# Two changes of shape: the bias network's second layer in column tiles, and self-attention without weight products

## The chip, the cores and the metric

The kernel runs on one core of a Trainium2 chip. The time is that of the device, in microseconds, and the time given for a kernel is the median of its runs. Everything is computed in 32-bit floats. TensorE multiplies matrices: it holds one operand (the weights[...]) and streams the other past it (here mostly 512 columns), and writes into PSUM, a memory of 8 banks of 128 partitions by 512 floats. VectorE (DVE), ScalarE (ACT) and GpSimd (POOL) do the other arithmetic, SyncE (SP) starts most transfers. Each engine works through its own queue[...].

## The reference

The input is x, two images of 512 channels by 32x32 points (1024 points). Two blocks follow one another. The first is a deformable attention with eight heads (groups) in each image, thus 16 pairs of image and head; each head has 64 channels and 64 sampled keys. What matters here is the bias that a small network computes for each pair of a query point (1024) and a key (64):

```
pos  = grid_q[:, :, None, :] - grid_kv[:, None, :, :]        # 2 numbers a pair
bias = sign(pos) * log1p(abs(pos))
bias = relu(bias @ cpb_w1 + cpb_b1)                          # 2 -> 128
bias = relu(bias @ cpb_w2 + cpb_b2)                          # 128 -> 128
bias = bias @ cpb_w3 + cpb_b3                                # 128 -> 1
sim  = (q k^T) * scale + bias
out  = softmax(sim) v                                        # then out_w, residual
```

An MLP (512 to 2048 to 512, gelu) with a residual ends the first block. The second block is self-attention over the 1024 points of an image with 512 channels and one head:

```
q, k, v = Wq x + bq,  Wk x + bk,  Wv x + bv
out     = x + Wp (softmax(q^T k / sqrt(512)) v) + bp
```

## The kernel before

It runs in five stages, all on one core: the preparation (queries, offsets, sampled keys, and the features `fea` of positions, which go to memory as `fdr` and come back spread over all partitions), the bias loop, the MLP, and the self-attention.

The bias loop is written for the 16 pairs of image and head, which the code calls groups. A step `s` deals with two keys (r and r+32 of the 64); there are 512 steps. The functions are:

- `st_tables` (L270 to L283) loads the features of 32 keys (`fb`) and makes two tables from them, `ta` on ScalarE and `tb` on GpSimd: the first layer's products with x and with y.
- `st_layer1` (L285) makes `h1`, 128 hidden units by 1024 points for one key, as the clamped sum of a column of `ta` and one of `tb`, one VectorE instruction for a key (L290). Four buffers.
- `st_layer2` (L299) multiplies `h1` by the 128x128 weights `cw2` into a tile of two banks (L304; two calls, one for each 512 points), and ScalarE takes it out with bias and relu as `h2` (L308). Three such tiles in PSUM.
- `st_layer3` (L312) sums over the 128 hidden units with `w3p` (L327). The weights are a window of 32 columns in which one column holds the weights and the rest are 0, so that each step's two keys land on their own partitions of `sim`; for two halves of the points and two keys there are four calls on four column tiles of 32. The first step of a group also multiplies queries and keys into the same bank (L317).
- `softmax_steps` (L333) turns a group's scores (`pt`, L339), normalises them on VectorE and ScalarE, turns them back (`pb`, L354) and multiplies by the values (`pa`, L361), in four parts that are spread over the loop by `due`.

The loop's order is written out by hand: in step s the first layer of step s+1, the second layer of s, and in every second step the third layer of the two steps before; a part of the softmax comes every second step. The tile framework puts the instructions in the engines' queues by the order of the text and by when it expects their inputs, so that an instruction can stand somewhat later than written, and it sets the semaphores.

The self-attention first multiplies weights by weights: `gw[0]` from Wq and Wk, `gw[1]` from Wv and Wp (`psg`, L460), and two bias vectors `ub` (`psu`, L469). Then, for each image, `qs` (`psp`, L484), values `vt` (`psv`, L493), scores against x itself (`pss`, L504), softmax, turning (`psx`, L523), and the output (`psa`, L544), which has Wp in it already.

Of the kernel before, what the change touches and what calls it, by code (L numbers as in the profile page):

```python
# [14 lines left out]
P = 128  # L15
# [5 lines left out]
R = 32  # L21
# [10 lines left out]
    ("bq", 4), ("bv", 4), ("bp", 4), ("dwb", 1), ("cb1", 1), ("cb2", 1), ("cb3", 1), ("w3", 1),  # L32
    ("w1x", 1), ("w1y", 1), ("dww", 36),
# [10 lines left out]
def conv_seq_kernel(ctx: ExitStack, tc: tile.TileContext, x, kst, cst, vec, wsm, outw, w1, w2, wl, out):  # L44
# [16 lines left out]
    def col(name, i=0):  # L61
        return vs[:, VOFF[name] + i : VOFF[name] + i + 1]
# [7 lines left out]
    w3p = cp.tile([P, 2 * R - 1], F32, name="w3p")  # L70
    nc.gpsimd.memset(w3p, 0.0)
    nc.gpsimd.tensor_copy(w3p[:, R - 1 : R], col("w3"))

    dp = ctx.enter_context(tc.tile_pool(name="dp", bufs=1, space=bass.MemoryType.DRAM))
    fdr = dp.tile([NG, 2, 2 * W, R], F32, name="fdr")
# [13 lines left out]
    with tc.tile_pool(name="ph", bufs=1) as ph, tc.tile_pool(name="ph2", bufs=2) as ph2, tc.tile_pool(  # L89
# [92 lines left out]
        for f in range(2):  # L182
# [12 lines left out]
        nc.vector.tensor_copy(  # L195
            kv.rearrange("p k b (e r) -> p (k b) r e", e=2), pk.rearrange("p (g r e) -> p g r e", r=R, e=2)
        )
# [45 lines left out]
        for c in range(2):  # L243
            nc.sync.dma_start(
                out=fdr[:, c, :, :].rearrange("g p j -> p g j"),
                in_=fea[0:64].rearrange("p f g (c j) -> p (f g) c j", c=2)[:, :, c, :],
            )
# [11 lines left out]
    with tc.tile_pool(name="lp", bufs=2) as lp, tc.tile_pool(  # L259
# [4 lines left out]
        NS = NG * R  # L264
        tabs, h1s, h2s, sims = {}, {}, {}, {}


        def st_tables(c):
            b, k, f = groups[c // 2]
            fb = lp.tile([P, 2, W, R], F32, name="fb", bufs=1)  # L270
            nc.sync.dma_start(
                out=fb.rearrange("p a x j -> p (a x j)"),
                in_=fdr[f * 8 + b * NCH + k, c % 2].rearrange("p j -> (p j)").partition_broadcast(P),
            )
            ta = lp.tile([P, R, W], F32, name="ta")
            tb = lp.tile([P, R, H], F32, name="tb")
            nc.scalar.activation(  # L277
                ta.rearrange("p j x -> p x j"), fb[:, 0], AF.Identity, bias=col("cb1"), scale=col("w1x")
            )
            nc.gpsimd.tensor_scalar(  # L280
                tb.rearrange("p j y -> p y j"), fb[:, 1], col("w1y"), 0.0, ALU.mult, ALU.add
            )
            tabs[c] = (ta, tb)  # L283

        def st_layer1(s):  # L285
            ta, tb = tabs[s // 16]
            for e in range(2):
                j = 2 * (s % 16) + e
                h1 = lp.tile([P, HW], F32, name="h1", bufs=4)
                nc.vector._custom_dve(  # L290
                    TENSOR_ADD_SAT,
                    out=h1.rearrange("p (y x) -> p y x", x=W),
                    in0=ta[:, j, :].unsqueeze(1).to_broadcast([P, H, W]),
                    in1=tb[:, j, :].unsqueeze(2).to_broadcast([P, H, W]),
                    s0=FMAX, s1=0.0,
                )
                h1s[s, e] = h1

        def st_layer2(s):  # L299
            for e in range(2):  # L300
                h1 = h1s.pop((s, e))
                ps = zp.tile([P, 2, 512], F32, name="ps2")
                for h in range(2):
                    nc.tensor.matmul(  # L304
                        ps[:, h, :], cw2, h1[:, h * 512 : (h + 1) * 512], start=True, stop=True
                    )
                h2 = lp.tile([P, 2, 512], F32, name="h2", bufs=6)
                nc.scalar.activation(h2, ps, AF.Relu, bias=col("cb2"))  # L308
                h2s[s, e] = h2

        def st_layer3(s):
            gi, r = divmod(s, R)  # L312
            b, k, f = groups[gi]
            if r == 0:
# [8 lines left out]
            h2 = [h2s.pop((s, e)) for e in range(2)]  # L323
            for h in range(2):
                for e in range(2):
                    q = 64 * h + 32 * e
                    nc.tensor.matmul(  # L327
                        sims[gi][q : q + 32, :], w3p[:, R - 1 - r : 2 * R - 1 - r], h2[e][:, h, :],
                        start=False, stop=(r == R - 1),
                    )  # L330

        def softmax_steps(gi):
            b, k, f = groups[gi]  # L333
            sim = sims.pop(gi)
            ss = lp.tile([P, 512], F32, name="ss")
# [7 lines left out]
            ex = lp.tile([P, 8, J], F32, name="ex")  # L343
# [11 lines left out]
            at = lp.tile([P, 512], F32, name="at")  # L355
# [14 lines left out]
        st_tables(1)  # L370
        st_layer1(0)
        for s in range(NS + 2):
            if s % 16 == 2 and s // 16 >= 1 and s // 16 + 1 < 2 * NG:
                st_tables(s // 16 + 1)
            if s + 1 < NS:
                st_layer1(s + 1)
            if s < NS:
                st_layer2(s)
            if s % 2 == 0 and s >= 2:
                st_layer3(s - 2)  # L380
                st_layer3(s - 1)
                if s % R == 0:
                    tail = softmax_steps(s // R - 1)
                    due = s
            if tail is not None and s >= due:
                tail = tail if next(tail, 0) is None else None
                due = s + 2
# [54 lines left out]

    wl_s = cp.tile([P, 4, NCH, C], F32, tag="big", name="wl_s")
# [4 lines left out]
    with tc.tile_pool(name="sp", bufs=1) as sp, tc.tile_pool(  # L448
        name="sps", bufs=2, space=PSUM
    ) as sps, tc.tile_pool(name="spm", bufs=4, space=PSUM) as spm:  # L450

        gw = sp.tile([P, 2, NCH, C], F32, name="gw")
        ub = sp.tile([P, 2, NCH], F32, name="ub")
        for i in range(2):
            for k in range(NCH):
                ps = spm.tile([P, 512], F32, tag="ps", name="psg")
                for o in range(NCH):
                    nc.tensor.matmul(  # L460
                        ps, wl_s[:, 2 * i, o, k * P : (k + 1) * P], wl_s[:, 2 * i + 1, o, :],
                        start=(o == 0), stop=(o == NCH - 1),
                    )
                nc.scalar.copy(gw[:, i, k, :], ps)
        for i, bn in enumerate(("bq", "bv")):
            for k in range(NCH):
                ps = spm.tile([P, 512], F32, tag="ps", name="psu")
                for o in range(NCH):
                    nc.tensor.matmul(  # L469
                        ps[:, 0:1], wl_s[:, 2 * i + 1, o, k * P : (k + 1) * P], col(bn, o),  # L470
                        start=(o == 0), stop=(o == NCH - 1),
                    )
                if i == 0:
                    nc.vector.tensor_copy(ub[:, i, k : k + 1], ps[:, 0:1])
                else:
                    nc.vector.tensor_tensor(ub[:, i, k : k + 1], ps[:, 0:1], col("bp", k), ALU.add)
        for b in range(B):
            qs = sp.tile([P, NCH, HW], F32, name="qs")
            for o in range(NCH):
                for h in range(2):  # L480
                    n = slice(h * 512, (h + 1) * 512)
                    ps = spm.tile([P, 512], F32, tag="ps", name="psp")
                    for k in range(NCH):
                        nc.tensor.matmul(  # L484
                            ps, gw[:, 0, k, o * P : (o + 1) * P], xs[:, k, b, n],
                            start=(k == 0), stop=(k == NCH - 1),
                        )
                    nc.scalar.activation(qs[:, o, n], ps, AF.Identity, bias=ub[:, 0, o : o + 1])
            vt = sp.tile([P, 8, C], F32, name="vt")
            for m in range(8):  # L490
                ps = spm.tile([P, 512], F32, tag="ps", name="psv")
                for k in range(NCH):
                    nc.tensor.matmul(  # L493
                        ps, xs[:, k, b, m * P : (m + 1) * P], gw[:, 1, k, :],
                        start=(k == 0), stop=(k == NCH - 1),
                    )
                nc.vector.tensor_copy(vt[:, m, :], ps)
            aT = sp.tile([P, 8, HW], F32, name="aT")

            def scores(t):  # L500
                ps = sps.tile([P, 2, 512], F32, name="pss")
                for h in range(2):
                    for k in range(NCH):
                        nc.tensor.matmul(  # L504
                            ps[:, h, :], qs[:, k, t * P : (t + 1) * P], xs[:, k, b, h * 512 : (h + 1) * 512],
# [32 lines left out]
            turn(7, before)  # L538
            for h in range(2):
                n = slice(h * 512, (h + 1) * 512)  # L540
                for o in range(NCH):
                    ps = spm.tile([P, 512], F32, tag="ps", name="psa")
                    for m in range(8):
# [3 lines left out]
                        )  # L547
                    res = sp.tile([P, 512], F32, name="res", bufs=3)
                    nc.vector.scalar_tensor_tensor(
                        res, ps, ub[:, 1, o : o + 1], xs[:, o, b, n], ALU.add, ALU.add  # L550
# [18 lines left out]
def _layout(np, inputs):  # L569
# [7 lines left out]
    def twice(v):  # L577
# [6 lines left out]
        "mb2": cols(L0["mlp_b2"]), "bq": cols(L1["bq"]), "bv": cols(L1["bv"]), "bp": cols(L1["bp"]),  # L584
        "dwb": twice(L0["off_dw_b"].reshape(DH, 1)), "cb1": L0["cpb_b1"].reshape(P, 1),
        "cb2": L0["cpb_b2"].reshape(P, 1), "cb3": np.broadcast_to(L0["cpb_b3"].reshape(1, 1), (P, 1)),
        "w3": L0["cpb_w3"].reshape(P, 1), "w1x": L0["cpb_w1"][0].reshape(P, 1),
# [25 lines left out]
    def rows(w):  # L613
        return w.reshape(w.shape[0] // P, P, w.shape[1]).transpose(1, 0, 2)

    wl = np.stack([rows(L1["Wq"]), rows(L1["Wk"]), rows(L1["Wv"]), lhs(L1["Wp"])], axis=1)
# [3 lines left out]
        "outw": lhs(L0["out_w"]), "w1": lhs(L0["mlp_w1"]), "w2": lhs(L0["mlp_w2"]), "wl": wl,  # L620
    }
# [20 lines left out]
```

## Time and profile before

| | |
|---|---|
| median of three runs | 3417.21 us (3415.55 to 3419.95) |
| profiled execution, its time | 3417.21 us |
| its span, first to last instruction | 3415.3 us |
| granted TensorE clock, mean | 0.990 |
| TensorE busy | 3346.8 us (98%) |
| VectorE busy | 1535.5 us (45%) |
| ScalarE busy | 1353.1 us (40%) |
| GpSimd busy | 75.7 us (2%) |
| preparation, up to the first second-layer matmul | 166.2 us |
| bias loop, up to the end of the third layer | 166.2 to 2509.9 us |
| last softmax, MLP | 2509.9 to 3020.6 us |
| self-attention | 3020.6 to 3415.3 us |

How to read it: a row of the costliest groups has the line of the code, the engine, the operation, the tile that is written and those that are read, the shape, the count, then busy time in us and the mean of one in ns, then how long the engine stood idle just before such instructions and what ended that. PE is TensorE's matmul, PEld its loading of weights, which lies beside matmuls. A shape such as `128*32 128x512` is 128 rows by 32 columns of weights, with 512 columns streamed. The mean of one matmul (about 600 ns) is longer than the time between two of them, since they are pipelined; busy time counts overlapping ones once. In a timeline a line is a start in us, a length in us, and what ran. In the chain told in order of time a line is a start, a length and a count, without the overlaps.

### The profile page before, as it was taken

To read this page: it belongs to the slowest core of one execution; us is meant where nothing else is said; L and a number is where in the kernel's file an instruction comes from. 1 tells how busy PE (TensorE), PEld (TensorE's weight loads), DVE (VectorE), ACT (ScalarE), POOL (GpSimd) and SP (SyncE) were. 2 spreads that over 40 slices of the span, in tenths; PEclk is the share of its full clock that TensorE was granted. 3 is DMA by queue.
4 is the path that set the end of the run, shared out by engine and by line. 5 is a ranking of instruction groups with operands and counts; after the bars stand their busy time and mean duration, and the time that the engine had idled before them with its cause. 6 is when DMAs were issued, how large, how long until landed. Compare 5 with 4: busy or idle time off the path is not lost.

```text
span 3415.3 us, 28243 instructions
## 1 busy us (share of the span) xinstructions
PE 3346.8 (98%) x11132; PEld 1339.9 (39%) x11132; DVE 1535.5 (45%) x1419; ACT 1353.1 (40%) x1273; POOL 75.7 (2%) x42
## 2 busy tenths in 40 slices
PE   8599999999999999999999999999999999999999
PEld 3333333333333333333333333333334444444444
DVE  2555555555555555555655555555520000002122
ACT  1355555555555555555555555555520100101010
POOL 0000000000000000000000000000000000000000
PEclk9799999999999999999999999999999999999999
DMA  1100000000000000000000000000020000100000
GB/s 63 53 25 13 13 13 13 25 13 13 13 13 13 25 13 13 13 13 13 25 13 13 13 13 13 25 13 1 1 86 0 0 0 0 49 0 0 25 0 25
DMA packets 14257, 58.77 MB, mean 17 GB/s; under 512 B 3376, under 2 KB 3632, under 8 KB 8880
## 3 DMA queue, kind: packets, MB, share of 16 engines
q1 hardware_dynamic: 13552, 55.84, 4.5%
q8 instruction: 90, 1.47, 0.2%
q10 hardware_dynamic: 576, 1.14, 0.1%
q14 instruction: 39, 0.32, 0.0%
HBM read 52.52 MB, written 4.46 MB: 17 GB/s over the span
## 4 chain that ended last, share of the span: by engine, by line
PE 98%; DVE 1%; ACT 1%; DMA 0%; issue 0%; ACTq 0%; SPq 0%; DVEq 0%
PE ps L304 53%; PE sim L327 14%; PE psm L433 6%; PE psh L425 6%; PE psa L544 3%; PE pss L504 3%; PE pc L139 2%; PE pso L409 2%; PE psp L484 2%; PE psv L493 2%; PE pa L361 1%; PE psg L460 1%; PE pkv L188 0%; PE psq L113 0%; PE sim L317 0%; PE psx L523 0%
## 5 line engine op out<-in xcount | busy, mean ns | idle before, releaser
L304 PE MATMUL ps<-h,kp 128*128 128x512 f32 x4096 | 1828.6, 599 | 12.5 <-DVE h L290 12.5
L290 DVE CUSTOM_DVE_ANT_1 h<-ta,tb 128x1024 f32<-128x1024 f32 x1024 | 1295.5, 1268 | 955.2 <-PE ps L304 943.8
L308 ACT ACTIVATE h<-ps,vs 128x1024 f32<-128x1024 f32 x1024 | 1136.1, 1113 | 1056.4 <-PE ps L304 1055.2
L304 PEld LDWEIGHTS ps<-h,kp 128*128 128x128 f32 x4096 | 756.6, 190 | 1064.6 <-issue 1050.3
L327 PE MATMUL sim<-h,w3p 128*32 128x512 f32 x4096 | 493.0, 598 | 0.0
L327 PEld LDWEIGHTS sim<-h,w3p 128*32 128x32 f32 x4096 | 107.2, 109 | 348.4 <-issue 348.1
L433 PE MATMUL psm<-hm,w_s 128*128 128x512 f32 x512 | 220.4, 592 | 0.0
L437 DVE SCALAR_TENSOR_TENSOR xs<-psm,vs,xs 128x512 f32<-128x512 f32 x16 | 12.0, 752 | 425.1 <-PE psm L433 425.1
L429 ACT ACTIVATE hm<-psh,vs 128x512 f32<-128x512 f32 x64 | 44.0, 687 | 377.7 <-PE psh L425 377.7
L425 PE MATMUL psh<-xn,w1b 128*128 128x512 f32 x384 | 165.5, 592 | 0.0
L433 PEld LDWEIGHTS psm<-hm,w_s 128*128 128x128 f32 x512 | 97.3, 190 | 122.5 <-issue 122.5
L280 POOL TENSOR_SCALAR tb<-fb,vs 128x1024 f32<-128x1024 f32 x32 | 73.7, 2302 | 2276.8 <-DVE h L290 2115.0
L504 PE MATMUL pss<-xs,qs 128*128 128x512 f32 x256 | 112.2, 592 | 0.0
L544 PE MATMUL psa<-aT,vt 128*128 128x512 f32 x256 | 111.1, 596 | 0.0
L425 PEld LDWEIGHTS psh<-xn,w1b 128*128 128x128 f32 x384 | 73.0, 190 | 91.8 <-issue 91.8
L277 ACT ACTIVATE ta<-fb,vs 128x1024 f32<-128x1024 f32 x32 | 77.5, 2421 | 36.5 <-DMA fb<-fdr 33.9
L544 PEld LDWEIGHTS psa<-aT,vt 128*128 128x128 f32 x256 | 48.9, 192 | 60.8 <-issue 60.8
L504 PEld LDWEIGHTS pss<-xs,qs 128*128 128x128 f32 x256 | 47.7, 190 | 55.5 <-issue 55.5
L514 ACT ACTIVATE ex<-pss,mx 128x1024 f32<-128x1024 f32 x16 | 17.8, 1113 | 124.6 <-DVE mx L511 124.6
L139 PE MATMUL pc<-qpad,dg 128*128 128x512 f32 x72 | 66.0, 1093 | 0.0
L409 PE MATMUL pso<-att,ow_s 128*128 128x512 f32 x128 | 58.3, 615 | 0.7 <-ACT att L365 0.7
L484 PE MATMUL psp<-xs,gw 128*128 128x512 f32 x128 | 57.0, 607 | 0.0
(102 smaller groups left out, 834.9 us busy)
## 6 DMA issues: line engine op xcount, KB each, us to landing
fb<-fdr SPq DMA_DIRECT2D x32, 1024.0 KB, 4.7
xs<-in_x SPq DMA_DIRECT2D x8, 512.0 KB, 7.7
w_s<-in_w SPq DMA_DIRECT2D x4, 1024.0 KB, 15.2
wl_s<-in_wl SPq DMA_DIRECT2D x4, 1024.0 KB, 8.0
out<-res SPq DMA_DIRECT2D x16, 256.0 KB, 2.0
w1b<-in_w SPq DMA_DIRECT2D x3, 1024.0 KB, 8.9
ow_s<-in_outw SPq DMA_DIRECT2D x1, 1024.0 KB, 6.2
w1a<-in_w SPq DMA_DIRECT2D x1, 1024.0 KB, 8.5
```

Of the source, the lines that this page charges most:

```text
L139: nc.tensor.matmul(pc.rearrange("p (g y x) -> p g y x", y=8, x=8), dg, qpad[:, :, ky : ky + 29 : 4, kx : kx + 29 : 4], start=(t == 0), sto ...
L277: nc.scalar.activation(ta.rearrange("p j x -> p x j"), fb[:, 0], AF.Identity, bias=col("cb1"), scale=col("w1x"))
L290: nc.vector._custom_dve(TENSOR_ADD_SAT, out=h1.rearrange("p (y x) -> p y x", x=W), in0=ta[:, j, :].unsqueeze(1).to_broadcast([P, H, W]), i ...
L304: nc.tensor.matmul(ps[:, h, :], cw2, h1[:, h * 512 : (h + 1) * 512], start=True, stop=True)
L308: nc.scalar.activation(h2, ps, AF.Relu, bias=col("cb2"))
L327: nc.tensor.matmul(sims[gi][q : q + 32, :], w3p[:, R - 1 - r : 2 * R - 1 - r], h2[e][:, h, :], start=False, stop=(r == R - 1),)
L409: nc.tensor.matmul(ps, ow_s[:, k, o * P : (o + 1) * P], att[:, k, b, n], start=(k == 0), stop=(k == NCH - 1),)
L425: nc.tensor.matmul(ps, w1i, xn2[:, k, :], start=(k == 0), stop=(k == NCH - 1),)
L433: nc.tensor.matmul(ps, w2_s[:, i, o * P : (o + 1) * P], hm[:, i, :], start=(i == 0), stop=(i == NF - 1),)
L484: nc.tensor.matmul(ps, gw[:, 0, k, o * P : (o + 1) * P], xs[:, k, b, n], start=(k == 0), stop=(k == NCH - 1),)
L504: nc.tensor.matmul(ps[:, h, :], qs[:, k, t * P : (t + 1) * P], xs[:, k, b, h * 512 : (h + 1) * 512], start=(k == 0), stop=(k == NCH - 1),)
L544: nc.tensor.matmul(ps, vt[:, m, o * P : (o + 1) * P], aT[:, m, n], start=(m == 0), stop=(m == 7),)
```

## The change

It does two things. In the bias loop a step now deals with two pairs of neighbouring keys. The second layer takes a pair: for each half `z` of the 128 hidden outputs (64 of them) and each half `h` of the points there are four calls with 32 columns of weights each, on four column tiles; tiles 0 and 1 stream the first key of the pair, tiles 2 and 3 the second. A bank pair of PSUM then holds 64 hidden units of the first key on partitions 0 to 63 and the same units of the second on 64 to 127. ScalarE takes the half z=0 out as `rx`, with bias and relu, and z=1 as `ry`, with bias, relu and a scale that is the size of the last layer's weight, whose sign is in `w3s`. The third layer sums `rx` with the weights `w3d` and `ry` with `w3s`, again in windows of 32 columns, with two columns filled, one for each key of the pair. A way to add `rx` and `ry` on VectorE first (`st_pair`) is in the text, but with `DIRECT = NSL` the test `paired` is never true. The tables hold 16 keys instead of 32, the features are written in four transfers instead of two, `h1` has six buffers instead of four, and the parts of the softmax come at every pair instead of every second step.

In the self-attention the products of weights go. `ks` is computed like `qs`, the scores are taken of `qs` and `ks`, the values have their bias added from `bvb`, and the output is taken out as `os_` and multiplied by Wp (`psf`).

```diff
-        def st_layer2(s):
-            for e in range(2):
-                h1 = h1s.pop((s, e))
+        def st_layer2(pair):
+            h1 = [h1s.pop((pair, t)) for t in range(2)]
+            for z in range(2):
                 ps = zp.tile([P, 2, 512], F32, name="ps2")
                 for h in range(2):
-                    nc.tensor.matmul(
-                        ps[:, h, :], cw2, h1[:, h * 512 : (h + 1) * 512], start=True, stop=True
-                    )
-                h2 = lp.tile([P, 2, 512], F32, name="h2", bufs=6)
-                nc.scalar.activation(h2, ps, AF.Relu, bias=col("cb2"))
-                h2s[s, e] = h2
+                    for q in range(4):
+                        c0 = 64 * z + 32 * (q % 2)
+                        nc.tensor.matmul(
+                            ps[32 * q : 32 * q + 32, h, :], cw2[:, c0 : c0 + 32],
+                            h1[q // 2][:, h * 512 : (h + 1) * 512], start=True, stop=True,
+                        )
+                if z == 0:
+                    rx = lp.tile([P, 2, 512], F32, name="rx", bufs=4)
+                    nc.scalar.activation(rx, ps, AF.Relu, bias=col("cb2a"))
+                else:
+                    ry = lp.tile([P, 2, 512], F32, name="ry", bufs=5)
+                    nc.scalar.activation(ry, ps, AF.Relu, bias=sc[:, 3:4], scale=sc[:, 1:2])
+            rxs[pair], us[pair] = rx, ry
...
+        def st_pair(pair):
+            if paired(pair):
...
-            h2 = [h2s.pop((s, e)) for e in range(2)]
-            for h in range(2):
-                for e in range(2):
-                    q = 64 * h + 32 * e
-                    nc.tensor.matmul(
-                        sims[gi][q : q + 32, :], w3p[:, R - 1 - r : 2 * R - 1 - r], h2[e][:, h, :],
-                        start=False, stop=(r == R - 1),
-                    )
+            for direct in (True, False):
+                if direct and paired(2 * s):
+                    continue
+                for h in range(2):
+                    for e in range(2):
+                        q = 64 * h + 32 * e
+                        src = rxs.pop(2 * s + e) if direct and h == 1 else (rxs if direct else us)[2 * s + e]
+                        nc.tensor.matmul(
+                            sims[gi][q : q + 32, :], (w3d if direct else w3s)[:, 30 - 2 * i : 62 - 2 * i],
+                            src[:, h, :], start=False, stop=(not direct and i == NSL - 1),
+                        )
...
-        for s in range(NS + 2):
...
-                due = s + 2
+        for p in range(2 * NS + 2):
+            if p % 8 == 1 and p // 8 + 1 < 4 * NG:
+                st_tables(p // 8 + 1)
+            if p + 2 < 2 * NS:
+                st_layer1(p + 2)
+            if p < 2 * NS:
+                st_layer2(p)
+            if 1 <= p <= 2 * NS:
+                st_pair(p - 1)
+            if p % 2 == 1 and p >= 3:
+                s = p // 2 - 1
+                st_layer3(s)
+                if s % NSL == NSL - 1:
+                    tail = softmax_steps(s // NSL)
+                    due = p
+            if tail is not None and p >= due:
                 tail = tail if next(tail, 0) is None else None
+                due = p + 1
...
-        gw = sp.tile([P, 2, NCH, C], F32, name="gw")
-        ub = sp.tile([P, 2, NCH], F32, name="ub")
...
+            ks = sp.tile([P, NCH, HW], F32, name="ks")
+            for i, (dst, bn) in enumerate(((qs, "bq"), (ks, "bk"))):
+                for o in range(NCH):
+                    for h in range(2):
...
+                                ps, wl_s[:, i, k, o * P : (o + 1) * P], xs[:, k, b, n],
...
-                            ps[:, h, :], qs[:, k, t * P : (t + 1) * P], xs[:, k, b, h * 512 : (h + 1) * 512],
+                            ps[:, h, :], qs[:, k, t * P : (t + 1) * P], ks[:, k, h * 512 : (h + 1) * 512],
...
+            os_ = sp.tile([P, NCH, HW], F32, tag="qs", name="os_")
...
+                    nc.scalar.copy(os_[:, o, n], ps)
+                for o in range(NCH):
+                    ps = spm.tile([P, 512], F32, tag="ps", name="psf")
+                    for k in range(NCH):
+                        nc.tensor.matmul(
+                            ps, wl_s[:, 3, k, o * P : (o + 1) * P], os_[:, k, n],
+                            start=(k == 0), stop=(k == NCH - 1),
+                        )
```

## The prediction

> **What bounds the kernel now.** I read the chain of waits, then the groups by line, and then single stretches in the timeline, in the windows and in the chain told in order of time.
>
> ```profile
> PE 98%; DVE 1%; ACT 1%; DMA 0%; issue 0%; ACTq 0%; SPq 0%; DVEq 0%
> ...
> L304 PE MATMUL ps<-h,kp 128*128 128x512 f32 x4096 | 1828.6, 599 | 12.5 <-DVE h L290 12.5
> L290 DVE CUSTOM_DVE_ANT_1 h<-ta,tb 128x1024 f32<-128x1024 f32 x1024 | 1295.5, 1268 | 955.2 <-PE ps L304 943.8
> L308 ACT ACTIVATE h<-ps,vs 128x1024 f32<-128x1024 f32 x1024 | 1136.1, 1113 | 1056.4 <-PE ps L304 1055.2
> ...
> L327 PE MATMUL sim<-h,w3p 128*32 128x512 f32 x4096 | 493.0, 598 | 0.0
> ```
>
> TensorE carries 98% of the chain, and VectorE and ScalarE spend about 950 and 1050 us waiting for L304. So only TensorE's time counts, and anything on the other engines is free until TensorE must wait for it. Each f32 matmul shows as two records (4096 for 2048 calls); I call each a pass. Three lines of the timeline, and two of the weight loads inside them from the stretch before, give the rhythm of the bias loop:
>
> ```profile
> 1526.52 7.13 PE L304 MATMUL ps<-h,kp 128*128 128x512 f32 x16
> 1533.58 1.93 PE L327 MATMUL sim<-h,w3p 128*32 128x512 f32 x16
> 1535.44 7.13 PE L304 MATMUL ps<-h,kp 128*128 128x512 f32 x16
> ...
> 1525.12 0.13 PEld L327 LDWEIGHTS sim<-h,w3p 128*32 128x32 f32 x4 [0.30 <-issue]
> 1525.55 0.13 PEld L327 LDWEIGHTS sim<-h,w3p 128*32 128x32 f32 x4 [0.30 <-issue]
> ```
>
> Four keys take 8.92 us (1526.52 to 1535.44): 16 full passes in 7.06 us, then 16 column-tile passes in 1.86 us. The weight loads of the tiles come in fours, 0.43 us apart: four column tiles run side by side in the time of one full pass. The time of one full pass, undisturbed, is in the chain in order of time:
>
> ```profile
> 2539.07 54.93 PE psh L425 x128
> ```
>
> 54.93/128 = 0.429 us. So 16 full passes and 4 groups of four would need 20 x 0.429 = 8.58 us; 0.34 us of each 8.92 is the change between the two array shapes, there and back.
>
> **What the Trainium skill says.** "TensorEngine Tiling (Array Packing)", section Key Properties, says that a change of tiling mode, not a mere change of tile, drains TensorE. The trace agrees: the 0.34 us above falls at the two changes. "TensorE: Matmul & The Clock Gate", Part 3, The mechanism, says that matmuls on different column tiles overlap, starting some 4 ns apart; the groups of four at 0.43 us agree. The Tiling page, PSUM Bottleneck, warns that tiling speeds TensorE and not evacuation. Here evacuation does not grow: two keys by 64 hidden units still fill 128 partitions, so L308's 1024 activations of 1113 ns stay 1024.
>
> **The bias loop, part by part.** Second layer: for a pair of keys 2 halves z x 2 h x 4 tiles = 16 calls, 32 passes; four keys 64 passes, 16 groups of four, 16 x 0.429. Third layer: `DIRECT = NSL` makes `paired` always false, so `st_pair` emits nothing and both `rx` and `ry` go through TensorE: 8 calls for four keys, 16 passes, 4 groups, as before. New period 8.58 us if the groups hold. There are 512/2 = 256 periods, so the shape changes give back 256 x 0.34 = 87 us.
>
> Can tiles be issued at that rate for long? 80 passes with 80 weight loads in 8.58 us is 107 ns for each pair of instructions. In the trace 211 such pairs of L188 go by in 12.43 us, 59 ns each, so issue is no bound. A burst of L327 has only four groups, so a small loss in a long run can't be excluded; nothing can be gained below 0.429. I take none, and keep +1% (22 us) as the high end; a loss beyond that is a rival.
>
> ScalarE needs 4 x 1.11 us and VectorE 4 x 1.27 us in 8.58: covered. The tables come 64 times in halves (ta about 1.25 us instead of 2.42) and their loads too: they lie in ScalarE's 1056 us and the DMA's idle time, and a chunk is asked for five pairs, some 21 us, ahead. If that cover were gone, each would cost TensorE about 4 us.
>
> **The group boundaries.** 16 times the scores of a group are turned, normalised and multiplied:
>
> ```profile
> 607.86 1.92 PE ps L304 x4
> 609.77 0.44 PE pt L339 x4
> 610.21 5.15 PE ps L304 x12
> ...
> 618.22 0.59 PE pb L354 x4
> ```
>
> From the first L304 (166.16) to the end of the last L327 (2509.9) a group takes 146.5 us, of which 16 x 8.92 = 142.7 is rhythm and 3.8 us boundary. Today the turning matmuls pt and pb stand next to L304 in L304's own shape. After the change their neighbours are 32 wide, so pt gains two shape changes, pb one, sim and the two pa one each; at 0.17 us (half of 0.34) that is 1.0 us. Next, pt is not placed at once: today it comes after two calls of L304, because ss must first be computed. Two calls of the new second layer are half a group of four, so the group is split and takes 2 x 0.86 instead of 0.86 us: +0.86 (nothing, if it falls between groups). Then there are two waits, because VectorE gets its work differently. Both h1 of a pair are set free together at the end of a second layer, 1.72 us before the third layer ends; two L290 of 1.23 us then hold VectorE until 0.9 us after it, and ss, today started at 0.14 us, comes 0.8 us later with pt behind it at the head of TensorE's queue: +0.8 (0 to 1). And pb, today due two steps later (8.6 us), is due at the next pair, 3.43 us of matmuls later. The chain ss, pt, mx, ex, Exp, sm, reciprocal, mult is 0.75 + 0.5 + 0.68 + 0.69 + 0.62 + 0.69 + 0.20 + 0.69 us with some 0.1 us between each, about 5.6 us, plus the 0.8; TensorE arrives about 5.9 us after the third layer: +0.6 (0 to 3). Behind pb wait the next pair's second layer and with it both other engines. Sum 1.0 + 0.9 + 0.8 + 0.6 = 3.3 us; bounds 0.8 to 5.5. Times 16: +53 us (13 to 88). The loop: -87 + 53 = -34.
>
> **The self-attention.** The weight products go, K and the output projection come back.
>
> ```profile
> 3020.58 27.73 PE psg L460 x64
> 3048.31 8.72 PE psu L469 x64
> 3057.03 29.21 PE psp L484 x64
> ...
> 3048.00:3057.00 9.00, 9.00 (x66) 8.85 (x64) 1.10 (x7) 0.58 (x1) 0.00 (x0) 0.80 0.01 2
> 3057.00:3061.00 4.00, 4.00 (x7) 1.76 (x7) 0.16 (x1) 0.00 (x0) 0.00 (x0) 0.60 0.00 0
> ```
>
> Removed: psg 27.73 us, psu 8.72, and what psu leaves behind: in the windows the granted clock (the column after POOL) falls to 0.80 and 0.60, and the first psp takes 29.21 where 64 x 0.429 = 27.47, so 1.74. Sum 38.2. Added for each image: ks, 8 tiles x 4 calls x 2 passes = 64 passes, 27.5 us; psf, 64 passes, 27.5 us; both images 109.9. They are on TensorE's path and nothing hides them. Net +71.7. Costed at nothing: the evictions to ks (0.69 us each, under 3.4 us of matmuls), the bias in vt (about 0.7 us as today), the load of bvb, and os_: the first three k of psf can run while its last quarter is copied. If dependencies are kept for the whole tile it costs under 1 us, four times at most.
>
> **The start.** Four writes of the features rather than two on SP (0.67 us of issue each), then a table load of half the size (perhaps 3.3 us, now 4.7) and half a ta (1.2 less); but the first group of four needs both h1 of the pair, 1.27 us more. Zero, within 3 us. The new scale columns are a few VectorE instructions of 0.17 us during the first loads.
>
> **Sum.** The profiled execution took 3417.21 us, which is also the median (span 3415.3 and 1.9 around it). -34 + 72 = +38: 3455 us.
>
> **Rivals.** (a) The boundaries grow little. The change is -15 + 16g, with g the growth of a boundary in us. With g between 0.5 and 1.4 it is within 0.2%, which is about what can be told from no change: 3417. For: TensorE's order is not fixed by the text (pt stands later than written), so an order without splits and waits is possible. Against: the shape changes alone are near 1.0. (b) The other side: faster. One mechanism: drains at the boundaries are as cheap as beside L304 today, so g stays below 0.5 and the 87 us outweighs the 72: 3402. Against: it needs pt and pb to cost nothing extra in a 32-wide neighbourhood. (c) Four streams don't keep 0.429 in long runs, for instance as two tiles read the same key at once, which no row shows: at 0.44 us a group it is 256 x 20 x 0.011 = 56 us more, 3511. (d) The passes of a call can't be grouped across four tiles in the second layer and only two run at once: 256 x 16 x 0.429 = 1757 more, 5210. L327 has the same call order and is grouped, so this is unlikely.
>
> **How the numbers follow.** The forecast 0.63, (a) 0.14, (b) 0.09, (c) 0.10, (d) 0.04. The forecast's own range is 3425 to 3485 (boundaries +21 to +76, the rest within a few us). The whole range reaches to the middle of (b) and (a) and to the nearer part of (c): 3412 to 3500. Faster is (b), 0.09; within 0.2% is (a), 0.14; the rest, 0.77, is slower.
>
> **What would show it.** A period of four keys of 8.58 us, with no gap between the second layer and the third; the second layer's weight loads in fours; group periods near 144 us with TensorE waits before pt and pb; 64 more passes for ks and psf in each image at 27.5 us. A period over 8.7 us would make (c) right; group periods under 141.5 us would make (b) right.

## The result, and the profile after

| | median | runs | ratio to before (95% interval) |
|---|---|---|---|
| before | 3417.32 us | 4 (3415.55 to 3419.95) | |
| after | 3444.78 us | 4 (3443.77 to 3445.3) | 1.0079 (1.0062 to 1.0097) |

The changed kernel is 27.5 us slower, 0.8%. The forecast was 38 us slower. The page of the changed kernel has these chain shares and groups:

```profile
PE 98%; DVE 1%; ACT 1%; DMA 0%; issue 0%; SPq 0%; ACTq 0%; DVEq 0%
...
L327 PE MATMUL ps<-h,kp 128*32 128x512 f32 x16384 | 1834.3, 593 | 12.1 <-DVE h L306 12.1
L306 DVE CUSTOM_DVE_ANT_1 h<-ta,tb 128x1024 f32<-128x1024 f32 x1024 | 1210.4, 1223 | 1012.0 <-PE ps L327 994.4
...
L333 ACT ACTIVATE rx<-ps,vs 128x1024 f32<-128x1024 f32 x512 | 570.0, 1113 | 704.5 <-PE ps L327 704.5
L336 ACT ACTIVATE ry<-ps,sc 128x1024 f32<-128x1024 f32 x512 | 614.7, 1201 | 246.3 <-PE ps L327 245.6
L366 PE MATMUL sim<-rx,w3d 128*32 128x512 f32 x2048 | 275.8, 593 | 0.0
L366 PE MATMUL sim<-ry,w3s 128*32 128x512 f32 x2048 | 275.5, 592 | 0.0
```

TensorE still bounds everything: 98% of the chain, and the other engines wait for L327. The second layer has four times the passes, 16384, in nearly the same busy time (1834.3 us, before 1828.6). That busy time is no measure of the gain: records are longer than the time between two starts, so busy time hides how closely they follow. The rhythm shows it. From the timeline of the changed kernel (start, length, what ran), first TensorE, then some of its weight loads:

```profile
1531.03 7.05 PE L327 MATMUL ps<-h,kp 128*32 128x512 f32 x64
1537.90 1.04 PE L366 MATMUL sim<-rx,w3d 128*32 128x512 f32 x8
1538.76 1.04 PE L366 MATMUL sim<-ry,w3s 128*32 128x512 f32 x8
1539.62 7.05 PE L327 MATMUL ps<-h,kp 128*32 128x512 f32 x64
...
1536.61 0.13 PEld L327 LDWEIGHTS ps<-h,kp 128*32 128x32 f32 x4 [0.30 <-issue]
1537.04 0.13 PEld L327 LDWEIGHTS ps<-h,kp 128*32 128x32 f32 x4 [0.30 <-issue]
1537.47 0.13 PEld L366 LDWEIGHTS sim<-rx,w3d 128*32 128x32 f32 x4 [0.30 <-issue]
1537.90 0.13 PEld L366 LDWEIGHTS sim<-rx,w3d 128*32 128x32 f32 x4 [0.30 <-issue]
```

Four keys take 8.59 us from start to start (8.583 as the mean of the whole periods in the trace), where 8.92 were needed. The fours of loads keep their 0.43 us across the border between the second and the third layer; nothing is lost there any more.

Where the rest went is at the group boundaries. The changed kernel's chain told in order of time, over one boundary:

```profile
599.97 1.29 PE sim L366 x12
601.26 1.70 PE ps L327 x10
602.96 0.59 PE pt L380 x4
603.54 6.14 PE ps L327 x54
609.68 1.00 PE sim L353 x2
610.68 0.59 PE pb L395 x4
611.27 1.00 PE sim L353 x2
612.27 1.85 PE sim L366 x16
614.12 1.00 PE pa L402 x2
615.12 3.57 PE ps L327 x32
618.69 1.00 PE pa L402 x2
619.69 3.57 PE ps L327 x32
```

There is no wait in it. But `pt` comes after five calls (10 passes) of the second layer, which is one group of four and one call alone, and `pb` stands between the two `sim` calls. In the kernel before, the two `sim` calls stood together:

```profile
615.36 1.01 PE sim L317 x4
```

There both took 1.01 us; here each takes 1.00 us. From one `pt` to the next the kernel before needs 146.53 us and this one 143.89 (the first and the last period apart). With the rhythm taken off (16 x 8.92 = 142.7 and 16 x 8.583 = 137.33) a boundary costs 3.83 us before and 6.56 after: it grew by 2.73 us.

By stages of the two profiled executions: from the first second-layer matmul to the self-attention's first matmul 2854.4 us before (166.16 to 3020.58) and 2807.8 after (167.29 to 2975.12), 46.6 less; the preparation 1.1 more; the self-attention 73.7 more.

### The profile page after: what moved, and what is told of

The parts are those of the page before. It is cut to its first block, busy times and chain, and to the rows that moved or that the text cites. A ratio compares the mean times of both kernels' runs of the same rounds, so it can differ in the third digit from the quotient of the medians.

```text
span 3443.5 us, 52325 instructions
## 1 busy us (share of the span) xinstructions
PE 3374.8 (98%) x23548; PEld 1200.9 (35%) x23548; DVE 1449.5 (42%) x1417; ACT 1411.5 (41%) x1329; POOL 81.7 (2%) x79
## 4 chain that ended last, share of the span: by engine, by line
PE 98%; DVE 1%; ACT 1%; DMA 0%; issue 0%; SPq 0%; ACTq 0%; DVEq 0%
PE ps L327 52%; PE sim L366 13%; PE psm L476 6%; PE psh L468 6%; PE psa L567 3%; PE psp L505 3%; PE pss L525 3%; PE pc L152 2%; PE pso L452 2%; PE psf L575 2%; PE psv L514 2%; PE pa L402 1%; PE sim L353 1%; PE pkv L201 0%; PE psq L126 0%; PE psx L544 0%
## 5 line engine op out<-in xcount | busy, mean ns | idle before, releaser
L327 PE MATMUL ps<-h,kp 128*32 128x512 f32 x16384 | 1834.3, 593 | 12.1 <-DVE h L306 12.1
L306 DVE CUSTOM_DVE_ANT_1 h<-ta,tb 128x1024 f32<-128x1024 f32 x1024 | 1210.4, 1223 | 1012.0 <-PE ps L327 994.4
L327 PEld LDWEIGHTS ps<-h,kp 128*32 128x32 f32 x16384 | 557.6, 110 | 1222.1 <-issue 1197.2
L333 ACT ACTIVATE rx<-ps,vs 128x1024 f32<-128x1024 f32 x512 | 570.0, 1113 | 704.5 <-PE ps L327 704.5
L336 ACT ACTIVATE ry<-ps,sc 128x1024 f32<-128x1024 f32 x512 | 614.7, 1201 | 246.3 <-PE ps L327 245.6
L366 PE MATMUL sim<-rx,w3d 128*32 128x512 f32 x2048 | 275.8, 593 | 0.0
L366 PE MATMUL sim<-ry,w3s 128*32 128x512 f32 x2048 | 275.5, 592 | 0.0
L525 PE MATMUL pss<-ks,qs 128*128 128x512 f32 x256 | 112.2, 592 | 0.0
L505 PE MATMUL psp<-xs,wl_s 128*128 128x512 f32 x256 | 110.3, 592 | 0.8 <-DVE xs L480 0.8
L292 ACT ACTIVATE ta<-fb,vs 128x512 f32<-128x512 f32 x64 | 84.2, 1315 | 38.9 <-DMA fb<-fdr 33.6
```

The lines of the kernel that those rows point to most:

```text
L292: nc.scalar.activation(ta.rearrange("p j x -> p x j"), fb[:, 0], AF.Identity, bias=col("cb1"), scale=col("w1x"))
L306: nc.vector._custom_dve(TENSOR_ADD_SAT, out=h1.rearrange("p (y x) -> p y x", x=W), in0=ta[:, j, :].unsqueeze(1).to_broadcast([P, H, W]), i ...
L327: nc.tensor.matmul(ps[32 * q : 32 * q + 32, h, :], cw2[:, c0 : c0 + 32], h1[q // 2][:, h * 512 : (h + 1) * 512], start=True, stop=True,)
L333: nc.scalar.activation(rx, ps, AF.Relu, bias=col("cb2a"))
L336: nc.scalar.activation(ry, ps, AF.Relu, bias=sc[:, 3:4], scale=sc[:, 1:2])
L366: nc.tensor.matmul(sims[gi][q : q + 32, :], (w3d if direct else w3s)[:, 30 - 2 * i : 62 - 2 * i], src[:, h, :], start=False, stop=(not dir ...
```

## Experiments

**The two halves alone.** One kernel has the changed bias loop with the old self-attention, the other the old loop with the new self-attention; each leaves out one half of the change, so no new code is shown.

> The changed bias loop with the self-attention of before (weight products kept). Theory: the loop gains 256 shape changes of 0.34 us and gives back 16 boundaries of 2.7 us, and nothing of the attention touches it: the same loop as in the changed kernel, 143.9 us a group, and about 3370 us in all. Rival: the attention's extra matmuls were partly hidden and the loop gained less, so that the loop alone stands nearer to 3400 us.

Measured: 3370.99 us (ratio 0.9864, 0.9849 to 0.9878), 143.89 us from pt to pt in every group but the last, as in the changed kernel. With before at 3417.86 in these runs the loop gains 46.9 us.

> The bias loop of before with the changed self-attention (ks and the output projection). Theory: 110 us of added passes less 38 us of weight products, all on TensorE's path, and up to 3 us of clock: 3489 to 3492 us. Rival (part of the added matmuls fills TensorE's waits): about 3460 us.

Measured: 3491.26 us (1.0214, 1.0199 to 1.0229), so +73.4. The halves add up to +26.5, and together they measured +27.5. Within that 1 us they don't disturb each other, and none of the added attention work is hidden.

**Fewer changes of shape without column tiles.** In the kernel before, the third layer runs every four steps. To make room, ss, ex and at get one buffer each; h2 gets nine.

```diff
-            if s % 2 == 0 and s >= 2:
-                st_layer3(s - 2)
-                st_layer3(s - 1)
+            if s % 4 == 0 and s >= 4:
+                for t in range(s - 4, s):
+                    st_layer3(t)
```

> The kernel before, with nothing of the change: full-width second layer, but the third layer runs for four steps at a time instead of two, which halves the changes between the two array shapes (128 fewer there and back). Theory (0.34 us is lost at each there-and-back): 128 x 0.337 = 43 us less, about 3374 us, and 16 passes of the second layer beside 8 calls of the third still at 0.429 us each. Rival (the 0.34 us belong to the third layer's calls, or to waits for the activations, not to the change of shape): unchanged, 3410 to 3420 us.

Measured: 3377.91 us (0.9884, 0.9869 to 0.9898), 40 us less. The timeline of this kernel:

```profile
708.58 14.00 PE L304 MATMUL ps<-h,kp 128*128 128x512 f32 x32
722.51 3.64 PE L327 MATMUL sim<-h,w3p 128*32 128x512 f32 x32
726.08 14.00 PE L304 MATMUL ps<-h,kp 128*128 128x512 f32 x32
```

Eight keys take 17.50 us from start to start, where two periods took 17.84: exactly one there-and-back of 0.34 us is gone. The layers' own work is the same, so the 0.34 us belong to the change of shape and not to the calls. The 3 us that are missing from 43 lie at the boundaries (144.09 us a group, where eight fewer there-and-back give 143.8).

**Uncut groups at the boundaries.** On top of the loop alone, first only the due step of the softmax parts (run after the other, and told first), then also `pt` one part later than `ss`. The due step:

```diff
-                due = p + 1
+                due = p + 2
```

> The loop alone with the softmax parts due every two pairs and nothing else: pb now stands behind the third layer, so the two sim calls run together again, while pt still cuts a group of four tile calls. Theory (the cut of the sim pair costs about 1.0 us a boundary, the cut of a group by pt about 0.7): 142.9 us a group, about 3355 us. Rival (only the cut by pt costs): 143.9 us a group, about 3370 us.

Measured: 3358.12 us (0.9825, 0.9808 to 0.9841), 143.03 us a group. This kernel's chain in order of time, from the second layer after pt on:

```profile
599.93 6.14 PE ps L327 x54
606.07 1.01 PE sim L353 x4
607.07 1.85 PE sim L366 x16
608.93 0.59 PE pb L395 x4
609.52 7.00 PE ps L327 x64
```

The two `sim` calls again take 1.01 us together, 0.99 us less than the two of 1.00. At its new place `pb` costs one more change of shape, so that the second layer behind it takes 7.00 us where others take 6.87. That makes 0.86 us less in a boundary, just as the period says (143.89 to 143.03).

And `pt` one part later as well:

```diff
             nc.vector.tensor_scalar(ss, sim, col("cb3"), None, ALU.add)
+            yield
             pt = mip.tile([P, 512], F32, tag="mi", name="pt")
```

> The loop alone, with the softmax parts due every two pairs and the turning pt one part later than ss, so that no group of four tile calls and no pair of sim calls is cut in two. Theory (a boundary's growth of 2.7 us is mostly two cuts, about 0.9 and 1.0 us): 141.9 us a group instead of 143.9, about 3339 us. Rival (the growth is the shape changes themselves): within 5 us of the loop alone, about 3368 us.

Measured: 3344.17 us (0.9784, 0.9767 to 0.98), 142.20 us a group, 26.8 us below the loop alone. This kernel's chain in order of time:

```profile
595.15 6.87 PE ps L327 x64
602.02 1.01 PE sim L353 x4
603.02 1.85 PE sim L366 x16
604.88 0.59 PE pt L381 x4
605.47 7.00 PE ps L327 x64
```

`pt` now stands between the layers, no group of four is cut, and that gives another 0.83 us. What is left of the growth, 142.20 - 137.33 - 3.83 = 1.04 us, is the shape changes. The chain bears this out: the second layer takes 7.00 us instead of 6.87 behind pt, pb and each of the two pa, the third layer 1.85 instead of 1.72 behind sim, pt takes 0.59 where it took 0.44 before, and the 0.19 us that the second layer behind pb was shorter before (6.87 against 7.06) are gone; together 0.99 us. The rival (the growth is shape changes alone) falls: they are 1.04 of 2.73.

**The order of the calls.** Neighbouring calls of the second layer share a tile, as the loops over q and h are exchanged (loop alone otherwise):

```diff
-                for h in range(2):
-                    for q in range(4):
+                for q in range(4):
+                    for h in range(2):
```

> The loop alone with the second layer's inner loops exchanged: both halves of the points on one tile, then the next tile, so that neighbouring calls of the second layer share a tile. Theory (tiles run side by side only when neighbouring calls are on different tiles): three to four passes of one tile go one after another, 20 to 28 us for the second layer of four keys instead of 6.9, and 6900 to 8700 us in all. Rival (the machine finds the overlap whatever the order of calls): 3371 us as with the loop alone.

Measured, in a single run: 3386.56 us. My theory falls by thousands of us. Its timeline, over a whole period and over the start of a boundary:

```profile
625.64 7.12 PE L327 MATMUL ps<-h,kp 128*32 128x512 f32 x64
632.51 1.11 PE L366 MATMUL sim<-rx,w3d 128*32 128x512 f32 x8
...
600.98 1.88 PE L327 MATMUL ps<-h,kp 128*32 128x512 f32 x4
602.79 0.66 PE L380 MATMUL pt<-kp,ss 128*128 128x128 f32 x4
```

64 passes still take 6.87 us (625.64 to 632.51): the four tiles run side by side although the text names one tile twice in a row. Whether TensorE takes passes of different tiles out of order, or something ahead of it reorders them, these runs don't prove. Two readings of this trace speak for TensorE. Ahead of `pt` the two calls run one after another, 4 passes in 1.81 us, as they must if they are on one tile as in the text; so there the text's order had not been changed. And within a group of four side by side the starts mostly lie 30 ns apart, where in the loop alone it is 7 ns: about four times as much, as if the four passes of each tile were taken up in a row before those of the next. Most of the 15.6 us lies at the boundaries (144.83 us a group, 0.94 more, times 15 is 14.1), where these two calls run alone. So this other order mattered only where the stream of tile calls is broken off.

**The end of the scores.** TensorE stands still once in each image of the self-attention. The windows of the changed kernel (stretch, its length, busy time and count of PE, PEld, DVE, ACT and POOL, granted clock, then the transfers):

```profile
3118.00:3121.00 3.00, 0.85 (x8) 0.61 (x6) 2.48 (x4) 1.01 (x1) 0.00 (x0) 1.00 0.00 0
3121.00:3124.00 3.00, 1.67 (x10) 1.27 (x11) 1.93 (x4) 0.20 (x2) 0.00 (x0) 0.91 0.00 0
3124.00:3127.00 3.00, 3.00 (x5) 1.20 (x4) 0.28 (x1) 0.00 (x0) 0.00 (x0) 0.52 0.00 0
```

TensorE waits for the last softmax of the image, and in the stretch after that the clock is granted at 0.52. In the kernel before, the first image has the same wait, and the clock stays at 1.00 (the turning after the wait, then the window behind it):

```profile
3178.25 1.07 PE L523 MATMUL psx<-kp,ex 128*128 128x128 f32 x8 [3.48 <-DVE ex L516]
...
3180.00:3183.00 3.00, 3.00 (x8) 1.33 (x7) 0.20 (x1) 0.00 (x0) 0.00 (x0) 1.00 0.00 0
```

The wait alone thus doesn't decide it. In two kernels the block that computes the values (psv) is moved from ahead of the scores to just before the last turning, `turn(7, before)`; nothing else is edited.

> The changed kernel with the values (psv) computed behind the last scores instead of ahead of the first, so that TensorE has work while the last softmax of an image is done. Theory (in each image TensorE stands 3.5 us there, and the clock that falls after it costs 1.7 us more in the first psa, which is the attention's excess over its passes): about 10 us less, 3434 us, psa in its full 27.5 us in both images. Rival (the lower clock at psa has another cause): 7 us less, 3438 us, psa still 29 us.

Measured: 3432.44 us (1.0043, 1.0029 to 1.0057), 12.3 us below the changed kernel. Its timeline at the same place, and before it that of the changed kernel:

```profile
3122.33 1.06 PE L544 MATMUL psx<-kp,ex 128*128 128x128 f32 x8 [3.48 <-DVE ex L537]
3123.23 29.33 PE L567 MATMUL psa<-aT,vt 128*128 128x512 f32 x64
```

```profile
3089.07 27.63 PE L554 MATMUL psv<-wl_s,xs 128*128 128x512 f32 x64
3116.53 1.04 PE L536 MATMUL psx<-kp,ex 128*128 128x128 f32 x8
3117.41 27.63 PE L567 MATMUL psa<-aT,vt 128*128 128x512 f32 x64
```

The wait of 3.48 us is gone, and `psa` takes its 27.5 us from start to start instead of 29.2. That is 5.2 us for each image. Between the two profiles the whole self-attention is 10.7 us shorter (468.4 to 457.7 us). Most of the rest, 2.4 us, lies in the preparation, which this edit doesn't touch; among the ten profiles here it takes 163.5 to 167.3 us.

The rival (another cause) falls as far as the wait is needed: in the two kernels without it no image loses clock here. But the traces of the eight kernels with it hold sixteen waits of 3.48 us, and six of these cost nothing further, the other ten 1.7 to 3.0 us. What decides between them stays open.

> The loop alone with uncut groups at the boundaries, and psv moved in the same way. Theory: about 10 us less than without the move, 3334 us, below both kernels. Rival: the moved psv delays the turning and the values, 3344 us or more.

Measured: 3335.73 us (0.9759, 0.9745 to 0.9774). This kernel, with the old attention, the column-tiled second layer, uncut boundaries and the moved psv, is 81.8 us faster than before and 109 us faster than after. The move gave 8.4 us here, not 10: without it only the first image had lost clock (1.7 us), so that 2 x 3.48 + 1.7 = 8.7 us were to be had.

## Why the prediction was right, point by point

- **What bounds.** TensorE alone, as said. ScalarE's ry became 88 ns dearer than rx (1201 and 1113 ns) and the tables came 64 times, and neither reached the time.
- **The period.** Forecast 8.58 us for four keys, measured 8.583; 256 x 0.336 = 86 us come back. Rival (c), four streams that don't keep pace, and rival (d), tiles that aren't grouped, are excluded by the same number. The reason I gave against (d), that L327 has the same call order, was not the right one: with another order of calls the groups were just as full.
- **The boundaries.** I had 3.3 us of growth and it is 2.73; as a sum of four terms it was right in two. Shape changes: 1.0 forecast, 1.04 measured. The cut by pt: 0.86 forecast, 0.83 measured. The two waits, 0.8 and 0.6: both zero. The step that failed here is "pt comes after two calls". It is placed after five, which covers the later ss (ss starts 0.78 us after the third layer where it was 0.14; I had worked out 0.9), and pb is placed in the pair of sim calls. So the place of the wait was filled with other TensorE work; the price for it, 0.86 us for the sim pair cut in two, I hadn't seen. That the sum came within 0.6 us of the growth is in part luck: 1.4 us of waits that weren't there stood in for 0.86 us that I had missed.
- **The loop as a sum.** -34 forecast; -46.9 in the loop alone. The growth falls due 15 times and not 16, since the last group has no second layer behind it that could be cut: 15 x 2.73 = 41.0, and -86 + 41 = -45, near the -46.6 between the two profiles.
- **The attention.** +71.7 forecast, +73.4 measured alone and 73.7 between the two profiles. The passes are as counted. The excess is the clock after the wait at the end of the scores: in the changed kernel's profile both images paid 1.7 us in `psa`, in that of before the first paid nothing and the second 1.7 us. The forecast held nothing for it. os_ cost nothing: psf starts where psa ends, without a gap (at 3152.39, that is 29.16 us after psa's 3123.23).
- **The total.** +38 forecast, +27.5 measured, so slower by less than I said. The term that was mis-sized is the boundaries (53 against 41 us): the two waits for the missed cut, 0.6 us a boundary, and 16 boundaries for 15. The attention's 2 us go the other way. The start was put at zero; the 1.1 us between the two profiles there are less than its scatter (163.5 to 167.3 us). Rival (a), boundaries that grow by 0.5 to 1.4 us, is what the uncut version became (1.04), and it was only to be had by moving pt and pb.

## What to carry to other kernels

Where two kinds of matmul alternate, count the changes of array shape: at 0.34 us for each there-and-back they were about 86 us here. Running more of one kind at a time took back 40 of them, and giving both kinds one shape all 86, less what the boundaries then cost. Once calls share the array in tiles, every instruction of another shape should stand between whole groups, since a call that is cut off from its group took the time of a whole group here (two passes, 0.86 us). When two changes come together, measure each alone: here a gain of 47 us was covered by a loss of 73.

## What was not expected of the hardware

- Four column tiles ran side by side at 0.43 us a group also when neighbouring calls in the text were on the same tile (a single run).
- Two 64x64 calls on different tiles took 1.01 us together and 1.00 us each when another instruction stood between them.
- A TensorE wait of 3.48 us was followed by a granted clock near 0.5 for about 3 us, worth 1.7 us; with work put into the wait this was gone. But six of sixteen such waits were followed by no loss.
- A relu on ScalarE with a scale taken per partition took 1201 ns, and without it 1113 ns.
